# A graph network of four layers: the second layer's outputs turned in squares of 32 and through DRAM

## The chip, the cores and the metric

The kernel runs on one core of one Trainium2 chip. The time is device microseconds of one execution. The engines are called as in the profile: PE is TensorE, DVE is VectorE, ACT is ScalarE, POOL is GpSimd, SP is the engine that here only issues DMAs.

## What is computed

Four attention layers over a graph of 4096 nodes with 256 features each, all in float32. Every layer ends in a residual addition and a layer norm. The change concerns the second one:

```python
def _L1_gnn_ref(x, edge, Wq, bq, Wk, bk, Wv, bv):
    NHEAD, HEAD_DIM = 4, 64
    q = _split_heads(x @ Wq + bq)
    k = _split_heads(x @ Wk + bk)
    v = _split_heads(x @ Wv + bv)
    mask = (edge.T.astype(jnp.float32) - 1.0) * 10000.0
    scores = jnp.einsum('hnd,hmd->hnm', q, k) / np.sqrt(HEAD_DIM)
    scores = scores + mask[None, :, :]
    attn = jax.nn.softmax(scores, axis=-1)
    ctx = jnp.einsum('hnm,hmd->hnd', attn, v)
    return ctx.transpose(1, 0, 2).reshape(x.shape[0], NHEAD * HEAD_DIM)

x = _layernorm(x + _L0_gnn_ref(x, adj, L0_gnn_W, L0_gnn_a), axis=-1)
x = _layernorm(x + _L1_gnn_ref(x, adj, L1_gnn_Wq, ...), axis=-1)
x = _layernorm(x + _L2_gnn_ref(x, adj, L2_gnn_W, L2_gnn_a), axis=-1)
x = _layernorm(x + _L3_gnn_ref(x, adj, L3_gnn_Wq, L3_gnn_Wk), axis=-1)
```

The kernel computes the masked softmax without its division first: weights are exp(score) times the 0/1 mask, their products with the values are summed, and the sums are divided by the row sums of the weights at the end.

## The kernel before

The features X (4096 rows of 256) stay in SBUF through all four layers. Each layer walks over 8 blocks of 512 query nodes (`NB`, `QW`), and inside a block over the keys.

In the second layer (`multi_head_attention`) a block has 64 units (`NH`) of 64 keys. All four heads of a unit are held in one tile of 128x1024: two heads by partition halves, two by column halves. The loop at L1014 runs over all 8 x 64 units, with a lag of three units between scores and sums. One turn i of it does this:

- `scores` (L852): eight PE matmuls of the 64x64 quarter arrays write the scores of unit i to a PSUM tile `p` (L867; three such tiles, of two banks each), and ACT takes exp in place (L869). Every fourth unit four DMAs on SP fetch the masks of four units, 8 bits each (L860; three such mask buffers).
- `weights` (L871): DVE multiplies `p` by the mask into `prob` in SBUF (L879; eight such tiles). For the row sums, even units are added to `den` by a POOL addition (L889) and odd ones by a DMA issued on POOL that accumulates (L895); units 1 and 3 are copied there by DMAs on SP (L893). In four units of a block (`relief`) DVE does POOL's addition (L996).
- `sums` (L897): eight PE matmuls add the products of unit i-3 with its values to `acc`, two PSUM banks with one set of buffers (L903). In a block's last unit ACT copies the first bank to the SBUF tile `kept0` (L908) and DVE the second to `kept1` (L909), so that the next block can use `acc`. In that turn the sums are issued ahead of the scores (L1016).
- `finish(b - 1, j)` (L965): one step of the ending of the block before, where j = i - 3.

A block's results lie with features on partitions and nodes along the columns, and they have to be turned before they can be added to X. The steps of `finish` are: 7 and 9, DVE joins the three parts of `den` (L912); 12, PE sums `den` over partitions into a `p` tile (L925) and ACT copies that to `kept2` (L928); 15, PE turns the row sums (L933) and the first two of four row groups of the outputs (L940) into a `p` tile, DVE takes reciprocals (L948), multiplies (L954) and adds to X (L957); 18, PE turns the other two row groups and DVE does the same; 21 to 41, layer norm. `halves` (L959) takes the next of the three `p` tiles for each of steps 12, 15 and 18.

PE, DVE and ACT run in the order in which the program is written (`manual_schedule`, L1013). SP and POOL are ordered by the planner, by when it expects an instruction to be ready. The eighth block's ending is done by `tail` (L1027) in the third layer.

The last layer already has another way of turning (`squares_far`, L1192): DVE transposes 32x32 squares (L1197), four DMAs on SP write them to DRAM, one from each 32 partitions, in pieces of 32 elements (L1201), and one DMA on SP reads them back with nodes on partitions (L1204).

Of the kernel before, what the change touches and what calls it, by code (L numbers as in the profile page):

```python
# [9 lines left out]
FP = mybir.dt.float32  # L10
# [8 lines left out]
P = 128  # L19
D = 256  # L20
KC = D // P
QB = 4
QW = QB * P
# [5 lines left out]
def kernel(  # L29
# [27 lines left out]
    nc = tc.nc  # L57
    N = x.shape[0]
    NT = N // P
    NB = N // QW  # L60

    def pool(stack, name, bufs, **kw):
        return stack.enter_context(tc.tile_pool(name=name, bufs=bufs, reuse_waits="tile", **kw))
# [58 lines left out]
    def turning_apart(squares, far, part, to, eng, between=False):  # L122

        B = P // QB
        squares = squares.tile([P, QB, KC, P], FP, name="squares")
        for c in range(KC):
            if c and between:
                yield
            nc.vector.transpose(squares[:, :, c, :].rearrange("p q (k n) -> p k q n", n=B),
                                part(c).rearrange("p k (q f) -> p k q f", f=B))  # L130
        yield
        far = far.tile([QB, B, QB, KC * P], FP, name="far")
        eng.dma_start(far.rearrange("a f q m -> (a f) (q m)"), squares.rearrange("p q c m -> p (q c m)"))
        yield
        to = to()
        for q in range(QB):
            eng.dma_start(to[q * B:(q + 1) * B], far[:, :, q, :].rearrange("a f m -> f a m"))
        return to.rearrange("p a (c m) -> p c a m", c=KC)

    def block_turning(sb, once, dr, rows, eng):  # L140
        to = lambda: sb.tile([P, KC * QW], FP, name="xT").rearrange("p (a m) -> p a m", a=QB)
        return turning_apart(once, dr, lambda c: rows[:, :, c * P:(c + 1) * P], to, eng)

    def at_once(steps):
        while True:
# [587 lines left out]
    def multi_head_attention(w_sb, b_sb, tail, rows_of_den, rows_done, narrow_edges, ga):  # L733
# [8 lines left out]
        MJ = 4  # L742
        NH = N // d
        W = KC * QW
        kept, den, rden, mvs, roots = {}, {}, {}, {}, {}
        with ExitStack() as lay:
            keep = pool(lay, "mh_keep", 1)
            kT = keep.tile([P, KC, N], FP, name="kT")
            qT = keep.tile([P, KC, N], FP, name="qT")
            V = keep.tile([P, NH, P], FP, name="V")  # L750
# [146 lines left out]
            def sums(b, j):  # L897
                if j == 0:
                    acc[b] = [pa.tile([P, QW], FP, name=f"acc{c}") for c in range(KC)]
                for r in range(KC):  # L900
                    for c in range(KC):
                        half = slice(c * d, (c + 1) * d)
                        nc.tensor.matmul(acc[b][c][r * d:(r + 1) * d, :], V[half, j, r * d:(r + 1) * d],  # L903
                                         prob[b, j][half, r, :], start=(j == 0), stop=(j == NH - 1))
                if j == NH - 1:

                    kept[b] = [fin1.tile([P, QW], FP, name=f"kept{c}") for c in range(KC)]
                    nc.scalar.copy(kept[b][0], acc[b][0])  # L908
                    (nc.scalar.copy if b == NB - 1 else nc.vector.tensor_copy)(kept[b][1], acc[b][1])  # L909

            def join_sums(b, n, eng=nc.vector):
                eng.tensor_tensor(den[b][:, 0, :], den[b][:, 0, :], den[b][:, n, :], OP.add)  # L912
# [1 line left out]
            def row_sums(bank, b):  # L914


                kept[b].append(fin1.tile([P, QW], FP, name=f"kept{KC}"))
                pds = [bank() for _ in range(KC)]
                for r in range(KC):
                    for s in range(2):  # L920
                        for c in range(KC):
                            g = 2 * r + s
                            half = slice(c * d, (c + 1) * d)
                            lo = r * QW + s * QW // 2
                            nc.tensor.matmul(pds[c][g * G:(g + 1) * G, :QW // 2], ones[half, :G],  # L925
                                             den[b][half, 0, lo:lo + QW // 2], start=True, stop=True)
                for c in range(KC):
                    nc.scalar.copy(kept[b][KC][:, c * QW // 2:(c + 1) * QW // 2], pds[c][:, :QW // 2])  # L928

            def turned_row_sums(bank, b):  # L930
                pd = bank()
                for k in range(QB):
                    nc.tensor.transpose(pd[:, k * P:(k + 1) * P], kept[b][KC][:, k * P:(k + 1) * P], ident)  # L933
                return pd

            def turned_half(bank, b, k):
                po = bank().rearrange("p (k f) -> p k f", f=D)
                for i in range(2):
                    for c in range(KC):
                        nc.tensor.transpose(po[:, i, c * P:(c + 1) * P],  # L940
                                            kept[b][c][:, (k + i) * P:(k + i + 1) * P], ident)
                return po

            def reciprocals(pd, b):
                rden[b] = fin.tile([P, QB, H], FP, name="rden4")
                parts = pd.rearrange("p (c k r s g) -> p k c r s g", c=KC, k=2, r=KC, s=2)
                for s in range(2):
                    nc.vector.reciprocal(rden[b][:, 2 * s:2 * s + 2, :].rearrange("p k (c r) -> p k c r", c=KC),  # L948
                                         parts[:, :, :, :, s, 0])
# [9 lines left out]
            def halves():  # L959

                p = ps.tile([P, KC, QW], FP, name="p")
                left = [p[:, r, :] for r in range(KC)]
                return lambda: left.pop(0)

            def finish(b, j):  # L965

                rows = [X[:, b * QB + k, :D] for k in range(QB)]
                if j in (7, 9):
                    join_sums(b, j // 2 - 2)
                elif j == 12:  # L970
                    row_sums(halves(), b)
                elif j == 15:
                    bank = halves()
                    pd = turned_row_sums(bank, b)
                    po = turned_half(bank, b, 0)
                    reciprocals(pd, b)
                    half(po, b, 0)
                elif j == 18:
                    half(turned_half(halves(), b, 2), b, 2)
                elif j in (21, 23, 25, 27):  # L980
                    k = (j - 21) // 2
                    if k == 0:
                        mvs[b] = fin.tile([P, QB, 2], FP, name="mv")
                    one_row(mvs[b], k, rows[k])
                elif j == 29:
                    roots[b] = begin_root(mvs[b])
                elif j == 31:

                    end_root(*roots[b], nc.gpsimd)
                    lift_mean(mvs[b], *roots[b][:2], nc.gpsimd)  # L990
                elif j in (35, 37, 39, 41):
                    k = (j - 35) // 2
                    scale_row(rows[k], mvs[b], roots[b][1], k)
                if j + LAG - 1 in relief:

                    nc.vector.tensor_tensor(*late.pop(), OP.add)  # L996
                    ga.dots(b * QB + relief.index(j + LAG - 1), (1,) if b > 1 else (0, 1))
                elif j == 57:
                    ga.factors(b)
                elif j == 59 and b == 0:  # L1000
                    ga.sources(b)
                elif j == 63 and b == 1:
                    ga.row(0, nc.sync)
                elif j == 33 and b == NB - 2:
                    nc.gpsimd.dma_start(ga.first_mask, adjT.rearrange("(t p) i -> p t i", p=P)[:, :QB, :QW])
# [131 lines left out]
    def cosine_attention(co, tail):  # L1137
# [4 lines left out]
        with ExitStack() as lay:  # L1142
# [48 lines left out]

            def squares_far(b, h, both):  # L1192

                B = P // QB
                sq = fin1.tile([P, QW], FP, name=f"kept{h}").rearrange("p (a k c s) -> p a k c s", a=QB, k=2, c=KC)
                for n, quarter in enumerate(both):
                    nc.vector.transpose(sq[:, :, :, n, :].rearrange("p a k s -> p k a s"),  # L1197
                                        quarter.rearrange("p (k a r) -> p k a r", k=2, r=B))
                away = far.tile([B, QB, QW // P, QB, B], FP, name="away")
                for q in range(QB):  # L1200
                    nc.sync.dma_start(away[:, :, :, q, :].rearrange("r a m s -> r (a m) s"),  # L1201
                                      sq[q * B:(q + 1) * B].rearrange("r a k c s -> r (a k c) s"))
                t = (fin1 if h else cp).tile([P, QW], FP, name="kept2")
                nc.sync.dma_start(t, away.rearrange("r a m q s -> a r (m q s)"))  # L1204
                back[b, h] = t.rearrange("p (k f) -> p k f", k=2)

            def outputs_far(b, step, seen):
# [241 lines left out]
```

## Time and profile before

| | |
|---|---|
| median of 3 runs | 2770.95 us (2770.05 to 2772.3) |
| the profiled execution, whole | 2767.94 us |
| its span, first to last instruction | 2766.2 us |
| second layer's loop, from its first to its last block | about 795 to 1693 us of the span |
| from block to block in it (copies of L908) | 112.55 us, between the second and the third 114.41 |
| granted TensorE clock | 1.0 throughout |
| L940, transposes of outputs in the loop | 56, by fours: 8 in each of seven blocks |
| L954, L957 in the loop | 14 each, 689 to 700 ns |
| L889, additions on POOL | 220, 2536 ns in the mean |
| DMAs of L895 on POOL | 240 of 512 KB, 5.3 us to landing |
| DMA engines, share of time in a block | 0.89 to 0.92 |

A row of the page's groups or of the timeline reads: start and duration in us (timeline), engine, line of the program, operation, what it writes and reads, shapes, count, and in brackets how long the engine was idle before and what ended that. The chain of waits is followed back from the last instruction: each row is the work that had to end for the next to begin. PE's ends are modelled, so the chain's distances say more than PE's busy time.

### The profile page before, as it was taken

To read this page: it belongs to the slowest core of one execution; us is meant where nothing else is said; L and a number is where in the kernel's file an instruction comes from. 1 tells how busy PE (TensorE), PEld (TensorE's weight loads), DVE (VectorE), ACT (ScalarE), POOL (GpSimd) and SP (SyncE) were. 2 spreads that over 40 slices of the span, in tenths; PEclk is the share of its full clock that TensorE was granted. 3 is DMA by queue.
4 is the path that set the end of the run, shared out by engine and by line. 5 is a ranking of instruction groups with operands and counts; after the bars stand their busy time and mean duration, and the time that the engine had idled before them with its cause. 6 is when DMAs were issued, how large, how long until landed. Compare 5 with 4: busy or idle time off the path is not lost.

```text
span 2766.2 us, 50216 instructions
## 1 busy us (share of the span) xinstructions
PE 2750.6 (99%) x19365; PEld 1443.0 (52%) x19365; DVE 2307.0 (83%) x3145; ACT 1702.2 (62%) x2668; POOL 1077.0 (39%) x1020
## 2 busy tenths in 40 slices
PE   9999999999999999999999999999999999999999
PEld 5333333333543333333333336888888777777776
DVE  8899999999777788887888889888888876677776
ACT  7899999999346666666666665565655422222222
POOL 0000000000049878788788796454455000000000
PEclk9999999999999999999999999999999999999999
DMA  8798898987449899898998988578778544454442
GB/s 236 149 188 186 195 197 188 196 184 163 99 120 192 179 193 187 187 188 185 194 186 187 195 176 211 157 202 211 194 192 236 108 75 77 76 81 80 76 73 42
DMA packets 279673, 445.48 MB, mean 161 GB/s; under 512 B 55321, under 2 KB 156169, under 8 KB 274442
## 3 DMA queue, kind: packets, MB, share of 16 engines
q0 software_dynamic: 108784, 216.29, 46.9%
q1 hardware_dynamic: 164280, 218.88, 26.6%
q10 hardware_dynamic: 6370, 7.10, 0.8%
q8 instruction: 152, 2.49, 0.3%
q14 instruction: 87, 0.71, 0.1%
HBM read 335.94 MB, written 39.40 MB: 136 GB/s over the span
## 4 chain that ended last, share of the span: by engine, by line
PE 94%; DVE 4%; ACT 1%; issue 1%; POOL 0%; DVEq 0%; ACTq 0%; POOLq 0%
PE acc L475 26%; PE acc L333 19%; PE p L867 16%; PE acc L903 16%; PE p L1163 4%; PE g L1163 3%; PE g L777 2%; DVE prob L323 2%; PE acc L482 1%; ACT prob L309 1%; PE g L635 1%; PE g L1108 1%; PE pv L797 1%; PE acc L215 1%; PE g L348 0%
## 5 line engine op out<-in xcount | busy, mean ns | idle before, releaser
L879 DVE TENSOR_TENSOR prob<-p,mask 128x1024 f32<-128x1024 f32 x512 | 619.1, 1221 | 163.2 <-ACT p L869 158.6
L869 ACT ACTIVATE p<-p,shift 128x1024 f32<-128x1024 f32 x512 | 555.6, 1088 | 319.5 <-PE p L867 318.1
L333 PE MATMUL acc<-prob,V 128*32 128x512 f32 x5888 | 638.8, 593 | 1.9 <-DVE prob L323 1.8
L889 POOL TENSOR_TENSOR den<-den,prob 128x1024 f32<-128x1024 f32 x220 | 558.0, 2536 | 89.9 <-DVE prob L879 85.3
L309 ACT ACTIVATE prob<-row,dst 128x512 f32<-128x512 f32 x892 | 557.9, 711 | 3.0 <-PE acc L333 2.7
L867 PE MATMUL p<-qT,kT 64*64 64x512 f32 x4096 | 531.1, 590 | 2.3 <-DVE prob L879 2.3
L903 PE MATMUL acc<-prob,V 64*64 64x512 f32 x4096 | 529.9, 589 | 0.0
L323 DVE SCALAR_TENSOR_TENSOR prob<-prob,mask 128x2048 f32<-128x2048 f32 x224 | 504.8, 2282 | 17.2 <-ACT prob L309 16.9
L333 PEld LDWEIGHTS acc<-prob,V 128*32 128x32 f32 x5888 | 188.7, 110 | 435.9 <-issue 405.2
L475 PE MATMUL acc<-mix,mixed 128*128 128x256 f32 x1476 | 401.4, 380 | 1.9 <-DVE quarters L497 1.0
L903 PEld LDWEIGHTS acc<-prob,V 64*64 64x64 f32 x4096 | 157.4, 133 | 282.2 <-issue 280.3
L475 PEld LDWEIGHTS acc<-mix,mixed 128*128 128x128 f32 x1476 | 278.5, 190 | 45.8 <-PE acc L475 3.1
L867 PEld LDWEIGHTS p<-qT,kT 64*64 64x64 f32 x4096 | 154.2, 133 | 279.3 <-issue 252.3
L1176 DVE TENSOR_TENSOR prob<-prob,mask 128x1024 f32<-128x1024 f32 x128 | 156.3, 1221 | 142.9 <-ACT prob L1167 142.9
L895 POOL DMA_DIRECT2D den<-prob x240 | 233.3, 972 | 62.6 <-DMA den<-prob 27.6
L475 PE MATMUL acc<-prob,X 128*128 128x256 f32 x984 | 252.8, 379 | 0.7 <-ACT quarters L489 0.7
L1095 POOL DMA_DIRECT2D mask<-in_adjT x64 | 47.7, 745 | 527.9 <-DVE prob L1176 509.1
L475 PEld LDWEIGHTS acc<-prob,X 128*128 128x128 f32 x984 | 186.6, 190 | 80.1 <-issue 59.2
L608 DVE SCALAR_TENSOR_TENSOR prob<-r,own,mask 128x512 f32<-128x512 f32 x252 | 177.0, 743 | 49.0 <-POOL mix L467 12.2
L1167 ACT ACTIVATE prob<-p 128x512 f32<-128x512 f32 x144 | 86.1, 598 | 212.4 <-PE p L1163 212.4
L320 POOL DMA_DIRECT2D den<-prob x24 | 21.1, 878 | 483.7 <-DVE prob L314 461.6
L1167 ACT ACTIVATE prob<-g 128x512 f32<-128x512 f32 x112 | 66.9, 597 | 199.2 <-PE g L1163 199.2
(246 smaller groups left out, 3046.9 us busy)
## 6 DMA issues: line engine op xcount, KB each, us to landing
mask<-in_adjT SPq DMA_DIRECT2D x254, 512.0 KB
den<-prob POOLq DMA_DIRECT2D x240, 512.0 KB, 5.3
den<-prob POOLq DMA_DIRECT2D x32, 1024.0 KB, 9.3
mask<-edges SPq DMA_DIRECT2D x512, 64.0 KB
mask<-in_adjT POOLq DMA_DIRECT2D x64, 512.0 KB, 5.7
edges<-in_adj POOLq DMA_DIRECT2D x32, 512.0 KB, 17.1
far<-squares SPq DMA_DIRECT2D x16, 512.0 KB
den<-prob SPq DMA_DIRECT2D x16, 512.0 KB
```

The source lines that it names most:

```text
L309: nc.scalar.activation(z[:, h, :], r, AF.Relu, bias=-1.0, scale=dst[:, j, h:h + 1])
L323: nc.vector.scalar_tensor_tensor(z, z, 1.0, mask[m][:, j % MJ, :].unsqueeze(1).to_broadcast([P, H, QW]), OP.add, OP.mult)
L333: nc.tensor.matmul(acc[b][h * G:(h + 1) * G, n, :], part, prob[b, j][:, h, :], start=(j == 0), stop=(j == NT - 1 and n < HC))
L475: nc.tensor.matmul(acc[at][:, half * HW:(half + 1) * HW], w, a, start=(g == 0 and n in (0, 2, 3, 5)), stop=(g == NP - 1), skip_group_check ...
L608: nc.vector.scalar_tensor_tensor(z[:, n, :], r, ga.own[:, j:j + 1], mask[:, n, :], OP.add, OP.mult)
L867: nc.tensor.matmul(p[c * d:(c + 1) * d, r, :], kT[half, c, at:at + d], qT[half, c, cols], start=True, stop=True)
L869: nc.scalar.activation(p, p, AF.Exp, bias=shift)
L879: nc.vector.tensor_tensor(z, p, mask[m][:, j % MJ, :].unsqueeze(1).to_broadcast([P, KC, QW]), OP.mult)
L889: nc.gpsimd.tensor_tensor(to, to, flat, OP.add)
L895: nc.gpsimd.dma_start(to, flat, accum_op=OP.add)
L903: nc.tensor.matmul(acc[b][c][r * d:(r + 1) * d, :], V[half, j, r * d:(r + 1) * d], prob[b, j][half, r, :], start=(j == 0), stop=(j == NH - 1))
L1163: nc.tensor.matmul(p.rearrange("p (k i) -> p k i", k=QB), T[j // QB][:, 0, j % QB], T[b][:, 1], start=True, stop=True)
```

## The change

For the first seven blocks of the second layer the outputs are turned as in the last layer. At a block's end ACT still copies the first bank of `acc`; in place of the second copy DVE transposes the second bank's squares, in two halves of the columns, straight from PSUM into two tiles (`kept1`, `kept2`). At steps 1 and 2 of `finish` DVE transposes the squares of `kept0`, one half each, into the same two tiles, and SP is given four DMAs to DRAM and one back for each half. At step 15 only the row sums are turned by PE. At steps 17 and 19 DVE multiplies and adds as before, with the tile that came back from DRAM in the place of the PSUM tile. Step 18 is gone. The row sums take the name `kept0`. The eighth block is done as before. In the last layer the same instructions are now made by the shared functions.

```diff
--- before.py
+++ after.py
@@ -140,6 +140,25 @@
     def block_turning(sb, once, dr, rows, eng):
         to = lambda: sb.tile([P, KC * QW], FP, name="xT").rearrange("p (a m) -> p a m", a=QB)
         return turning_apart(once, dr, lambda c: rows[:, :, c * P:(c + 1) * P], to, eng)
+
+    def squares_of(t):
+        return t.rearrange("p (a k c s) -> p a k c s", a=QB, k=2, c=KC)
+
+    def turn_squares(sq, n, quarter):
+
+        nc.vector.transpose(sq[:, :, :, n, :].rearrange("p a k s -> p k a s"),
+                            quarter.rearrange("p (k a r) -> p k a r", k=2, r=P // QB))
+
+    def put_far(far, sq):
+        B = P // QB
+        away = far.tile([B, QB, QW // P, QB, B], FP, name="away")
+        for q in range(QB):
+            nc.sync.dma_start(away[:, :, :, q, :].rearrange("r a m s -> r (a m) s"),
+                              sq[q * B:(q + 1) * B].rearrange("r a k c s -> r (a k c) s"))
+        return away
+
+    def fetch(t, away):
+        nc.sync.dma_start(t, away.rearrange("r a m q s -> a r (m q s)"))
 
     def at_once(steps):
         while True:
@@ -742,9 +761,11 @@
         MJ = 4
         NH = N // d
         W = KC * QW
-        kept, den, rden, mvs, roots = {}, {}, {}, {}, {}
+        HW = QW // 2
+        kept, den, rden, mvs, roots, squares, back = {}, {}, {}, {}, {}, {}, {}
         with ExitStack() as lay:
             keep = pool(lay, "mh_keep", 1)
+            far = pool(lay, "mh_turned", 2, space=bass.MemoryType.DRAM)
             kT = keep.tile([P, KC, N], FP, name="kT")
             qT = keep.tile([P, KC, N], FP, name="qT")
             V = keep.tile([P, NH, P], FP, name="V")
@@ -904,9 +925,16 @@
                                          prob[b, j][half, r, :], start=(j == 0), stop=(j == NH - 1))
                 if j == NH - 1:
 
-                    kept[b] = [fin1.tile([P, QW], FP, name=f"kept{c}") for c in range(KC)]
+                    if b == NB - 1:
+                        kept[b] = [fin1.tile([P, QW], FP, name=f"kept{c}") for c in range(KC)]
+                        for c in range(KC):
+                            nc.scalar.copy(kept[b][c], acc[b][c])
+                        return
+                    kept[b] = [fin1.tile([P, QW], FP, name="kept0")]
                     nc.scalar.copy(kept[b][0], acc[b][0])
-                    (nc.scalar.copy if b == NB - 1 else nc.vector.tensor_copy)(kept[b][1], acc[b][1])
+                    squares[b] = [squares_of(fin1.tile([P, QW], FP, name=f"kept{1 + h}")) for h in range(2)]
+                    for h in range(2):
+                        turn_squares(squares[b][h], 1, acc[b][1][:, h * HW:(h + 1) * HW])
 
             def join_sums(b, n, eng=nc.vector):
                 eng.tensor_tensor(den[b][:, 0, :], den[b][:, 0, :], den[b][:, n, :], OP.add)
@@ -914,7 +942,7 @@
             def row_sums(bank, b):
 
 
-                kept[b].append(fin1.tile([P, QW], FP, name=f"kept{KC}"))
+                total = kept[b, "den"] = fin1.tile([P, QW], FP, name=f"kept{0 if b < NB - 1 else KC}")
                 pds = [bank() for _ in range(KC)]
                 for r in range(KC):
                     for s in range(2):
@@ -925,12 +953,12 @@
                             nc.tensor.matmul(pds[c][g * G:(g + 1) * G, :QW // 2], ones[half, :G],
                                              den[b][half, 0, lo:lo + QW // 2], start=True, stop=True)
                 for c in range(KC):
-                    nc.scalar.copy(kept[b][KC][:, c * QW // 2:(c + 1) * QW // 2], pds[c][:, :QW // 2])
+                    nc.scalar.copy(total[:, c * QW // 2:(c + 1) * QW // 2], pds[c][:, :QW // 2])
 
             def turned_row_sums(bank, b):
                 pd = bank()
                 for k in range(QB):
-                    nc.tensor.transpose(pd[:, k * P:(k + 1) * P], kept[b][KC][:, k * P:(k + 1) * P], ident)
+                    nc.tensor.transpose(pd[:, k * P:(k + 1) * P], kept[b, "den"][:, k * P:(k + 1) * P], ident)
                 return pd
 
             def turned_half(bank, b, k):
@@ -965,18 +993,21 @@
             def finish(b, j):
 
                 rows = [X[:, b * QB + k, :D] for k in range(QB)]
-                if j in (7, 9):
+                if j in (1, 2):
+                    h = j - 1
+                    turn_squares(squares[b][h], 0, kept[b][0][:, h * HW:(h + 1) * HW])
+                    away = put_far(far, squares[b][h])
+                    t = fin1.tile([P, QW], FP, name=f"kept{1 + h}")
+                    fetch(t, away)
+                    back[b, h] = t.rearrange("p (k f) -> p k f", f=D)
+                elif j in (7, 9):
                     join_sums(b, j // 2 - 2)
                 elif j == 12:
                     row_sums(halves(), b)
                 elif j == 15:
-                    bank = halves()
-                    pd = turned_row_sums(bank, b)
-                    po = turned_half(bank, b, 0)
-                    reciprocals(pd, b)
-                    half(po, b, 0)
-                elif j == 18:
-                    half(turned_half(halves(), b, 2), b, 2)
+                    reciprocals(turned_row_sums(halves(), b), b)
+                elif j in (17, 19):
+                    half(back.pop((b, (j - 17) // 2)), b, j - 17)
                 elif j in (21, 23, 25, 27):
                     k = (j - 21) // 2
                     if k == 0:
@@ -1191,17 +1222,11 @@
 
             def squares_far(b, h, both):
 
-                B = P // QB
-                sq = fin1.tile([P, QW], FP, name=f"kept{h}").rearrange("p (a k c s) -> p a k c s", a=QB, k=2, c=KC)
+                sq = squares_of(fin1.tile([P, QW], FP, name=f"kept{h}"))
                 for n, quarter in enumerate(both):
-                    nc.vector.transpose(sq[:, :, :, n, :].rearrange("p a k s -> p k a s"),
-                                        quarter.rearrange("p (k a r) -> p k a r", k=2, r=B))
-                away = far.tile([B, QB, QW // P, QB, B], FP, name="away")
-                for q in range(QB):
-                    nc.sync.dma_start(away[:, :, :, q, :].rearrange("r a m s -> r (a m) s"),
-                                      sq[q * B:(q + 1) * B].rearrange("r a k c s -> r (a k c) s"))
+                    turn_squares(sq, n, quarter)
                 t = (fin1 if h else cp).tile([P, QW], FP, name="kept2")
-                nc.sync.dma_start(t, away.rearrange("r a m q s -> a r (m q s)"))
+                fetch(t, put_far(far, sq))
                 back[b, h] = t.rearrange("p (k f) -> p k f", k=2)
 
             def outputs_far(b, step, seen):
```

## The prediction

> **What bounds the kernel now.** I read the page's busy table first, then the stretches of the second layer block by block, then the chain of waits inside one block, then the timeline around the instructions that the change touches.
>
> ```profile
> PE 2750.6 (99%) x19365; PEld 1443.0 (52%) x19365; DVE 2307.0 (83%) x3145; ACT 1702.2 (62%) x2668; POOL 1077.0 (39%) x1020
> ```
> ```profile
> 1131.00:1244.00 113.00, 113.00 (x1064) 40.62 (x1060) 93.46 (x99) 71.66 (x72) 92.47 (x65) 1.00 0.90 187
> ```
>
> TensorE (PE) is busy for 99% of the span; the second row is one block of the second layer (busy times in the order PE, weight loads, DVE, ACT, POOL, then granted clock, DMA share, GB/s). PE fills it; VectorE and GpSimd each have 20 us free in 113. A microsecond taken off PE here is a microsecond of the kernel, as long as no other engine makes PE wait.
>
> ```profile
> 932.41 0.86 PE p L867 x8
> 933.27 0.86 PE acc L903 x8
> 934.13 0.59 PE p L933 x4
> 934.72 0.44 PE p L940 x4
> 935.15 1.02 PE p L867 x8
> ...
> 940.46 0.59 PE p L940 x4
> 941.05 1.02 PE p L867 x8
> ```
>
> In the chain every unit of 64 keys is 0.86 us of scores and 0.86 of sums, 1.716 together; 64 of them are 109.85. The copies of L908 start 112.55 us apart in most blocks; the other 2.7 us are the three visits of the previous block's ending (steps 12, 15, 18), two of which are shown.
>
> **What it removes.** At step 15 four transposes of outputs (0.44 us); the four of the row sums stay and keep their start-up. At step 18 the whole visit: 0.59, and the 1.02 - 0.86 = 0.16 by which the scores after it are longer: 0.75. Together 1.19 us a block. Seven blocks change (the last keeps the old way): 7 x 1.19 = 8.3 us off PE. The trace has these transposes at 0.44 us for four, 0.11 each, as they overlap. [...]
>
> **What it adds on VectorE's half of the boundary.** The 0.68 us copy of acc1 (L909) becomes two transposes of 128x256 out of PSUM. No row shows that; L1197 transposes the same size out of SBUF in 0.43, a pair of them in 0.76, and the copy shows that reading PSUM costs 0.68 for 512 columns. Bounds 0.72 and 1.1; I take 0.8. The copy ended at 906.34 and PE's first sums into acc began at 906.59, so 0.25 us hide it: the loss is 0 to 0.17 a block, 0 to 1.2 in all. I take 0; with the cover gone each 0.1 us costs 0.7. At steps 1 and 2 a transpose of 0.43 joins a unit in which VectorE is busy 1.22 of 1.716: 1.65, which fits. Behind it waits the next mask multiplication (L879), with 1.55 us to spare (below). ACT keeps its copy of acc0.
>
> **What it adds on SP and the DMA engines.** Ten DMAs a block. The last layer does the same today:
>
> ```profile
> 2230.74 5.37 SPq L1201 DMA_DIRECT2D away<-kept  x6
> 2237.80 0.60 SPq L1204 DMA_DIRECT2D kept<-away  x1
> 2245.58 0.56 SPq L1204 DMA_DIRECT2D kept<-away  x1
> ```
>
> Eight writes at 0.63 us and two reads at 0.56 are 6.2 us of issuing. Each read waits on SP until its writes have landed, and from the first write to the end of the second read 15.4 us pass. POOL's queue gets none. Behind a read on SP are the mask loads; L879 waits for these. Three mask buffers of four units each mean that a mask is asked for when unit j ends and needed nine units later, 15.4 us. Where it queues behind both reads it is asked for about 15.4 - 3 x 1.716 = 10.3 us late; the four mask issues take about 2 and a landing about 5.3 (that of the den DMAs on the page), so it is between 8 us early and 2.2 us late. I take 0, as the first read goes out after 7 us and SP can issue masks before the second. The turned rows are wanted 16 and 18 units (27 and 31 us) after the first write, and the reads go out 7 and 15 us after it; with 5.3 for a landing 11 us or more cover them, and past that VectorE stands still. On the DMA engines the queue of these transfers took 27.7% of the 16 us from 2230, 4.4 us of all sixteen for all the writes and one read; 5.3 with the other. The block leaves 10% of 113, some 11 us, idle. I take 0 here too.
>
> **What it moves, and where I see the price.** The two multiplications by the reciprocals and the two additions to X (L954, L957) now run at steps 17 and 19, and their input is no longer PSUM but a tile in SBUF. So each has two inputs in SBUF. Today they ignore GpSimd:
>
> ```profile
> 935.97 2.35 POOL L889 TENSOR_TENSOR den<-den,prob 128x1024 f32<-128x1024 f32 x1 [0.34 <-DMA den<-prob]
> 936.03 0.70 DVE L954 TENSOR_TENSOR p<-p,rden 128x512 f32<-128x512 f32 x1
> 936.77 0.69 DVE L957 TENSOR_TENSOR X<-p,X 128x512 f32<-128x512 f32 x1
> ```
>
> With a PSUM input both take their 0.7 while L889 runs. VectorE instructions with two SBUF inputs don't:
>
> ```profile
> 1769.89 0.42 DVE L652 SCALAR_TENSOR_TENSOR e<-e,h 128x256 f32<-128x256 f32 x1
> 1770.12 0.77 POOL L466 TENSOR_TENSOR mix<-prob,mix 128x256 f32<-128x256 f32 x1 [2.60 <-DVE mix L465]
> 1770.34 0.83 DVE L653 TENSOR_TENSOR y<-X,e 128x256 f32<-128x256 f32 x1
> ...
> 1711.30 2.88 DVE L912 TENSOR_TENSOR den<-den 128x1024 f32<-128x1024 f32 x2
> 1711.45 1.64 POOL L466 TENSOR_TENSOR mix<-prob,mix 128x256 f32<-128x256 f32 x1 [0.62 <-DVE mix L465]
> ```
>
> L653 takes 0.42 where GpSimd rests and 0.83 here: GpSimd came during L652, went first when L652 ended, and L653 waited. Two L912 at 1.22 should take 2.4 and took 2.88, with L466 between them. So GpSimd, once waiting, goes between two such instructions of VectorE. [...]
>
> Steps 17 and 19 run in units 20 and 22, even units, and L889 is issued in every even unit: in the timeline it starts 0.16 us after the end of that unit's L879 (time t), as after 940.36 and 944.55. The multiplication starts before it, holds it until t + 0.60, and L889 then needs 2.22 more (at 921.42 it took 3.20 and ended 2.22 after an L912 that was ahead). The addition ends 0.56 later (a held L912 ended 1.09 after L889 instead of taking 1.22, so 0.69 - 0.13), and the next L879 1.12 after that: t + 4.50, instead of t + 1.716. What PE forgives shows where this happened once:
>
> ```profile
> 1033.12 2.96 POOL L889 TENSOR_TENSOR den<-den,prob 128x1024 f32<-128x1024 f32 x1
> 1033.74 3.43 DVE L912 TENSOR_TENSOR den<-den 128x1024 f32<-128x1024 f32 x1
> ...
> 1038.36 1.09 PE L867 MATMUL p<-qT,kT 64*64 64x512 f32 x8 [1.01 <-DVE prob L879]
> ```
>
> The unit's L879 should have ended at 1033.82 + 1.716 = 1035.54; the scores that wait for its buffer would have begun at 1035.45 + 1.716 = 1037.17, so 1.55 us are free (0.08 is the signal). Step 17 thus costs 4.50 - 1.716 - 1.55 = 1.23 us. Then L879 of unit 22 ends at t + 5.64, the second half goes the same way to t + 5.64 + 4.50 = t + 10.14, against 3 x 1.716 + 1.55 + 1.23 = 7.93: 2.21 more. Together 3.44 a block. Check: that third block lasted 114.41 instead of 112.55, 1.86 for one such wait; two would be 3.7. I take 3.45. Without the wait VectorE would be at most 1.3 us late, under the 1.55.
>
> **The sum.** 7 x (3.45 - 1.19) = +15.8 us on the profiled span of 2766.2: 2782.0, and 2783.7 with the 1.7 us that lie around it in that execution (2767.94). The median of the runs, 2770.95, stands 3 us above it, so 2787.
>
> **Rivals.** (1) *VectorE keeps the way to SBUF*, or GpSimd arrives over 1.3 us after t and finds both instructions done. Then 2770.95 - 8.3 = 2763, faster. For it: multiplication and addition are issued 0.06 us apart or overlapping, and DMA traffic may hold GpSimd back (it waited 27.6 us for den DMAs in 17 places). Against: every one of the 28 L653 into y took 0.83, and L889 starts 0.16 after t in every block at units 20 and 22. It decides once GpSimd's delay is over 1.3 us. (2) *Masks behind the reads on SP*, on top of the forecast: 2.2 x 7 = 15 us more, 2802. For it: DMA share 0.9, so writes may land later than in the last layer. Against: in the third block SP stood still for 11.5 us at its start, and the block lost 1.86 in all. (3) *Only one half of two is hit*: 7 x (1.23 - 1.19) = 0.3, 2771, no change.
>
> **Chances.** Forecast 66%, rival 1 17%, rival 2 13%, rival 3 4%. The likeliest has its own range of 2780 to 2794 (3.4 to 3.7 a block and 0 to 1.2 at the boundary, with some spread of runs). The range 2762 to 2802 takes in most of rival 1 and the nearer half of rival 2. Some 0.2% (5.5 us) is what a measurement here can tell: slower 0.79, same 0.04, faster 0.17.
>
> **What would show it.** Right: L954 at 0.7, L957 near 2.8 us in the seven blocks, L889 between them, PE idle behind L879 at units 24 and 26, blocks some 114.8 us apart; no L940 in them. Wrong: L957 at 0.7 and blocks 111.4 apart (rival 1); L879 waiting for mask DMAs at units 16 to 20 (rival 2). What fails first, if I am wrong, is the turn GpSimd takes between the two instructions.

## The result, and the profile after

The changed kernel takes 2856.88 us (median of 5 runs, 2852.89 to 2862.0) against 2770.05 (5 runs beside it, 2769.27 to 2772.3): 1.0314 times as long, 95% interval 1.0302 to 1.0326. The prediction was 2787, with a range of 2762 to 2802. The profiled execution took 2856.88 us, its span is 2855.1: 88.9 us more than the 2766.2 before, and 87.7 of them lie in the second layer's seven changed blocks. In the table below, "score interval n" is the time from the first score matmul of unit n of a block to that of unit n+1 (1.716 us undisturbed), summed over the seven blocks, after less before.

| score interval | after less before, 7 blocks | in one block, before and after |
|---|---|---|
| 14 | +57.2 us | 1.72, and 9.1 to 11.6 |
| 15, 16 | +14.2 | 2.42 for interval 15, and 4.0 to 4.7 |
| 23, 25 | +23.3 | 1.72 each, and 2.91 and 3.85 |
| 18, 21 | -8.0 | 2.85 and 2.41, and 2.41 and 1.72 |
| all others | +1.0 | |

So the seven blocks paid what the prediction priced (23.3 for the two additions to X, 8.0 saved), and 71 us that it had put at nothing. On the page and in the busy times of one block (granted clock, DMA share and GB/s are the last three columns) PE now stands still for 11 us of the block, and the clock is no longer 1.00:

```profile
PE 2761.0 (97%) x19309; PEld 1447.8 (51%) x19309; DVE 2344.1 (82%) x3166; ACT 1702.7 (60%) x2668; POOL 1086.4 (38%) x1020
```
```profile
1278.34:1402.83 124.49, 113.65 (x1048) 41.22 (x1044) 98.65 (x103) 71.24 (x72) 93.77 (x66) 0.97 0.86 177
1308.53:1315.36 6.83, 3.17 (x16) 0.80 (x16) 4.45 (x4) 1.09 (x1) 3.07 (x1) 0.50 0.41 95
```

**Interval 14.** In the timeline of that block, VectorE has finished unit 11 at 1301.32 and then waits 9.60 us for a mask DMA before it can multiply unit 12 (L900); PE stands still 7.88 us behind it.

```profile
1300.10 1.22 DVE L900 TENSOR_TENSOR prob<-p,mask 128x1024 f32<-128x1024 f32 x1
1310.91 1.22 DVE L900 TENSOR_TENSOR prob<-p,mask 128x1024 f32<-128x1024 f32 x1 [9.60 <-DMA mask<-edges]
```
```profile
1312.19 1.98 PE L888 MATMUL p<-qT,kT 64*64 64x512 f32 x8 [7.88 <-DVE prob L900]
```

The waits of L900 over the whole second layer say that it is so in every changed block (before the change, no mask DMA stands among them). In the first of the seven the profile names a write, `away<-kept`, for the 9.4 us; there too a load for units 12 to 15 landed at 931.84, and L900 began at 932.01:

```profile
its engine sat idle before it (us, times) until:
  ACT p L890: 144.6, 262
  DMA mask<-edges: 57.8, 7
  DMA away<-kept: 9.4, 1
```

SP's timeline shows which load it is. Three of the four loads for units 12 to 15 go out at 1287.87; the fourth is queued behind six writes, the first read and two writes, and goes out at 1300.85. It lands 10 us later, at 1310.79. From the first write to the end of the second read's issue 21.3 us pass (15.4 in the last layer).

```profile
1287.87 1.96 SPq L881 DMA_DIRECT2D mask<-edges  x3
1289.93 6.69 SPq L156 DMA_DIRECT2D away<-kept  x6
1297.96 0.56 SPq L161 DMA_DIRECT2D kept<-away  x1
1298.57 2.24 SPq L156 DMA_DIRECT2D away<-kept  x2
1300.85 6.34 SPq L881 DMA_DIRECT2D mask<-edges  x3
1310.64 0.58 SPq L161 DMA_DIRECT2D kept<-away  x1
```

**Interval 15.** The window 1308.53 to 1315.36 above has a granted clock of 0.50. It begins inside the stall and outlasts it by 3.2 us: PE's first eight score matmuls behind the stall take 1.98 us together, where eight took 1.07 ahead of it. Such a stretch comes with each of the seven stalls, for 6.83 or 10.24 us.

**Intervals 23 and 25** are the wait for GpSimd that the prediction forecast; the expectations below call it the lock. L982 (before: L954) takes 0.68, GpSimd's L910 comes, and L985 (before: L957), which took 0.69, takes 2.72 to 2.73 in all 14 cases:

```profile
1327.30 0.68 DVE L982 TENSOR_TENSOR kept<-kept,rden 128x512 f32<-128x512 f32 x1
1327.54 2.65 POOL L910 TENSOR_TENSOR den<-den,prob 128x1024 f32<-128x1024 f32 x1 [0.76 <-DVE prob L900]
1328.01 2.73 DVE L985 TENSOR_TENSOR X<-kept,X 128x512 f32<-128x512 f32 x1
...
1331.93 1.09 PE L888 MATMUL p<-qT,kT 64*64 64x512 f32 x8 [1.01 <-DVE prob L900]
```

### The profile page after: what moved, and what is told of

Read it like the earlier page. It is cut to its first block, busy times and chain, and to the rows that moved or that the text cites. A ratio compares the mean times of both kernels' runs of the same rounds, so it can differ in the third digit from the quotient of the medians.

```text
span 2855.1 us, 50229 instructions
## 1 busy us (share of the span) xinstructions
PE 2761.0 (97%) x19309; PEld 1447.8 (51%) x19309; DVE 2344.1 (82%) x3166; ACT 1702.7 (60%) x2668; POOL 1086.4 (38%) x1020
## 5 line engine op out<-in xcount | busy, mean ns | idle before, releaser
L900 DVE TENSOR_TENSOR prob<-p,mask 128x1024 f32<-128x1024 f32 x512 | 616.1, 1220 | 215.8 <-ACT p L890 144.6
L910 POOL TENSOR_TENSOR den<-den,prob 128x1024 f32<-128x1024 f32 x220 | 576.0, 2618 | 134.5 <-DVE prob L900 123.0
L888 PE MATMUL p<-qT,kT 64*64 64x512 f32 x4096 | 541.9, 598 | 78.9 <-DVE prob L900 78.9
L924 PE MATMUL acc<-prob,V 64*64 64x512 f32 x4096 | 538.6, 595 | 0.0
L924 PEld LDWEIGHTS acc<-prob,V 64*64 64x64 f32 x4096 | 163.9, 134 | 282.7 <-issue 281.9
L916 POOL DMA_DIRECT2D den<-prob x240 | 239.9, 1000 | 94.5 <-DVE prob L900 41.6
L339 POOL DMA_DIRECT2D den<-prob x24 | 21.1, 878 | 483.9 <-DVE prob L333 461.8
L484 DVE TENSOR_TENSOR mix<-prob 128x512 f32<-128x512 f32 x246 | 179.4, 729 | 7.9
```

The lines of the kernel that those rows point to most:

```text
L484: nc.vector.tensor_tensor(s[:, :2, :], z[:, 0, :].rearrange("p (h i) -> p h i", h=2), z[:, :, HW:], OP.subtract)
L888: nc.tensor.matmul(p[c * d:(c + 1) * d, r, :], kT[half, c, at:at + d], qT[half, c, cols], start=True, stop=True)
L900: nc.vector.tensor_tensor(z, p, mask[m][:, j % MJ, :].unsqueeze(1).to_broadcast([P, KC, QW]), OP.mult)
L910: nc.gpsimd.tensor_tensor(to, to, flat, OP.add)
L916: nc.gpsimd.dma_start(to, flat, accum_op=OP.add)
```

## The experiments

The first four runs take the two costs apart. "Halves" are the two pairs of L982 and L985.

**a_no_trip**: no DMA of the trip; the squares are added where they lie.

```diff
-                    away = put_far(far, squares[b][h])
-                    t = fin1.tile([P, QW], FP, name=f"kept{1 + h}")
-                    fetch(t, away)
-                    back[b, h] = t.rearrange("p (k f) -> p k f", f=D)
+                    back[b, h] = squares[b][h].rearrange("p a k c s -> p (a k c s)").rearrange("p (k f) -> p k f", f=D)
```

> Leaves out the trip through DRAM of the seven blocks (eight writes and two reads each): the two halves multiply and add the squares as VectorE left them, so outputs of the second layer are not in their places. Theory (the extra time is two things: some 9.5 us a block of waiting for masks that SP and the DMA queue bring late because of the trip, with the clock drop that follows it, and 3.3 us a block of the two additions that wait for GpSimd): only the second stays; blocks 114.7 us apart, scores late at units 24 and 26 by 1.2 and 2.1 as now, no clock drop, median 2770 + 7 x (3.3 - 1.2) = 2785. Rival (VectorE's four transposes a block, or the longer hold of the accumulator at the boundary, make masks and scores late): those are still there, so the waits at units 12 to 15 stay and the time is over 2830.

Measured: 2795.93 us, 1.0084 (1.0068 to 1.0101). No mask is waited for; intervals 23 and 25 are 2.90 and 3.85 in six of the seven blocks, as in the change. The undisturbed blocks last 114.83 us (the prediction's 112.55 + 3.45 - 1.19 = 114.81); others up to 116.96, with intervals 23, 24, 26 or 27 longer and three dips of the clock of 3.41 us. These make the seven blocks 20.4 us longer than before in the profiled execution, where the expectation had 14.7. The time is 11 us over the expectation; the rest of that lies between runs (the kernel before took 3 us more beside this run than beside the change). The trip is what costs the other 61 us.

**b_odd_steps**: the halves one turn earlier, in units 19 and 21, when GpSimd is inside an addition instead of about to start one.

```diff
-                elif j in (17, 19):
-                    half(back.pop((b, (j - 17) // 2)), b, j - 17)
+                elif j in (16, 18):
+                    half(back.pop((b, (j - 16) // 2)), b, j - 16)
```

> The changed kernel with the two halves at steps 16 and 18 instead of 17 and 19, that is in odd units, in which GpSimd is given no addition. Theory (an addition of GpSimd goes between VectorE's multiplication and addition, and only that costs): the multiplication waits some 0.9 us for the rest of the addition of the unit before, the second instruction takes 0.7; VectorE is then at most 1.4 us late, under the 1.55 that are free, and the 3.3 us a block go: 2857 - 23 = 2834. Rival (two times 1.4 us more on VectorE within three units are too much whatever GpSimd does): 2850 or more.

Measured: 2844.52 us, 1.0262 (1.0247 to 1.0278). The stalls at 23 and 25 are gone, 0.7 us at interval 24 is left. Now the multiplication is what waits (0.81 in the first half, 2.00 in the second), and every addition takes 0.69. The stall at interval 14 stays (9.7 to 12.3). The time is 10 us over the 2834 of the theory: the profile has 5.0 of them at interval 24 and 3.4 at interval 14.

**c_ahead**: masks asked for eight units earlier in the program. (`ask` holds the four loads that stood in `scores`.)

```diff
+                n = b * NH + j
                 if j % MJ == 0:
...
+                    for u in range(0, 3 * MJ, MJ) if n == 0 else (n + 2 * MJ,):
+                        if u < len(units):
+                            ask(*units[u])
```

> The changed kernel with each group of masks asked for eight units earlier in the program, so that the planner puts all four loads of the fourth group ahead of the writes on SP; the fourth load of the fifth group then stands behind the second read. Theory A (the order on SP: one load of the fourth group behind eight writes and a read): the 9.5 us a block at unit 12 go, the fifth group comes in time or at most 2 us late, 2857 - 66 = 2791 to 2805. Theory B (the writes' packets are slow to drain beside the den DMAs, and whatever stands behind them on the queue is late): the wait moves to unit 16 and keeps half of its size or more, 2820 or more.

Measured: 2883.28 us, 1.0402 (1.0386 to 1.0417), worse. All loads for units 12 to 15 are now ahead of the writes, and interval 14 is 1.72; but three of the loads for units 16 to 19 are behind the first read and the fourth is behind the second, and interval 18 is 11.8 to 16.7. What stands behind the trip is late, whichever group it is.

**h_ahead_later_odd**: c_ahead, the reads written at steps 8 and 10, the halves at 16 and 18.

> Masks asked for eight units earlier, the reads given to SP at steps 8 and 10 instead of 1 and 2, so that the fifth group of masks is ahead of both, and the halves at steps 16 and 18. Theory (late masks and GpSimd's addition are all that the change costs): what is left is the work taken off PE, 1.2 us in each of seven blocks, 2770 - 8 = 2762. Rival (the trip loads the DMA engines so that den DMAs or masks come late in any order): 2770 or more, with VectorE or GpSimd waiting for DMAs.

Measured: 2824.37 us, 1.0187 (1.0172 to 1.0202). Interval 22 is now the long one, 5.2 to 10.4 us; in two blocks interval 18 is 4.5 and 4.7. The order alone doesn't mend it: the loads land late. In the fourth changed block the four loads for units 20 to 23 go out right behind the two reads, at 1297.88 to 1299.36, and land at 1311.5 to 1312.1; VectorE waits for them from 1307.91 to 1312.24.

The next four asked why. The trip writes 4,096 pieces of 128 bytes a block. **i_512** keeps the number of the DMAs and their order in the program and writes pieces of 512 bytes; the features come back in another order within a row, which the views of the two additions undo.

```diff
-        away = far.tile([B, QB, QW // P, QB, B], FP, name="away")
+        away = far.tile([B, QB, QB, P], FP, name="away")
         for q in range(QB):
-            nc.sync.dma_start(away[:, :, :, q, :].rearrange("r a m s -> r (a m) s"),
-                              sq[q * B:(q + 1) * B].rearrange("r a k c s -> r (a k c) s"))
+            nc.sync.dma_start(away[:, :, q, :], sq[q * B:(q + 1) * B].rearrange("r a k c s -> r a (k c s)"))
...
+        nc.sync.dma_start(t, away.rearrange("r a q m -> a r (q m)"))
```

> The pieces of the writes are 512 bytes long instead of 128 (1,024 a block instead of 4,096, as many DMAs, in the same places); the order of the features within a row is straightened by views of the two additions and a copy of the reciprocals. Theory D, the small pieces are slow to drain beside the row sums' accumulations and everything behind them on the queue is late: the trip takes 12 us or less instead of 20.7, the masks of the fourth group land nearly in time, score interval 14 falls from 9-11.6 us to 4 or less, no stretch at half clock follows, and the time is about 2795 (2785 to 2808), the stalls of about 1.2 and 2.1 us at intervals 23 and 25 staying. Theory E, what counts is the number of DMAs and their order (eight writes and two reads ahead of the masks, each with its issue and its place among the few that may be under way): interval 14 stays over 7 us and the time over 2835.

Measured: 2871.19 us, 1.0357 (1.0332 to 1.0382). Theory D falls. (The stall is at interval 18, 12.2 to 14.3 us: the planner put all loads for units 12 to 15 ahead of the reads here, and those for 16 to 19 behind both.)

**j_512_all** (i_512 with the orders of h_ahead_later_odd, halves at 16 and 20) and **o_512_odd** (i_512, halves at 16 and 20):

> Pieces of 512 bytes, masks asked for eight units earlier, reads at steps 8 and 10, halves at steps 16 and 20. Theory D: no mask is late, intervals 23 and 25 are near 1.72, and the time is about 2768 (2760 to 2778), so equal to the kernel before or a little faster. Theory E: a stall of 5 us or more remains in each block, as it did with the small pieces at interval 22, and the time is near 2820.

> The 512-byte pieces with the order of the change, and the halves at steps 16 and 20. Theory D and the lock together: run i_512 less 7 x (1.2 + 2.1 - 0.7) = 18, so about 2777 (2768 to 2790). Theory E: run b_odd_steps, 2844, within 10.

Measured: 2840.92 us, 1.0238 (1.0223 to 1.0253), and 2851.8, 1.0278 (1.0263 to 1.0293). Both keep the stall, at interval 18 (10.4 to 16.3 us, and 12.1 to 13.8). Theory E's numbers held to 21 and 8 us, but it gave no reason why a load should take 10 us to land.

**e_no_trip_odd**: a_no_trip with the halves of b_odd_steps.

> The trip left out (the second layer's outputs are added unturned across partitions), the halves at steps 16 and 18: neither the masks nor the addition of GpSimd stand in the way. If mask lateness and the lock are all that the change costs, this is the kernel before less what TensorE is spared: run a_no_trip, 2796, less 7 x 2.6 = 18, less its dips, about 2772 (2762 to 2780), no score interval over 3.5 us. A third cost that neither explains would show as a time over 2785.

Measured: 2769.81 us, 0.9988 (0.9979 to 0.9998), blocks of 112.16 to 112.18 us but for one (114.67; 114.41 before). Without the trip, and with 0.7 us a block of the wait for GpSimd left at interval 24, the change is worth 0.1%; no third cost is there.

The reason was in the packets and landings of the traces so far. While a read runs (in the change, until 2 us behind the issue of the next mask load, so that no other packets of this size mix in), we can count how many of its 2,048-byte packets are under way at one time:

```
packets of a read under way at once              most      mean while any is   us, first to last
after, first read of the 7 blocks                5 to 7    3.3 to 4.0          1.4 to 3.4
i_512, the same, whole                           6         2.8 to 3.9          4.1 to 4.9
before, the last layer's 14 reads                5 to 7    3.0 to 4.0          2.9 to 4.0
u_512_flat (below), first read of the 7 blocks   15 to 20  6.0 to 10.8         1.1 to 1.9
```

and when the sixteen parts of a DMA land, for three DMAs of SP's queue in the block shown above (the two writes behind the first read, and the mask load that VectorE waited for):

```
twelve parts                 the other four
1303.81 to 1304.26           1307.05 to 1310.19
1304.21 to 1304.90           1309.89 to 1310.57
1304.54 to 1305.16           1310.08 to 1310.79
```

The read's own semaphore shows it most directly. A write or a mask load counts sixteen landings. Each of the 28 such reads in the change's trace, and each of the 14 in the trace before, has five counts: one about 1 us behind its issue, and four landings (1306.65 to 1307.70 for the first read of the block shown). In u_512_flat and p_read4 below, the second layer's reads count sixteen.

So we take a read of 256 KB to lie on four of the sixteen DMA engines, 32 of its 128 packets of 2,048 bytes on each, among the row sums' packets of 4,096 bytes (about 340 ns each); the traces do not name a packet's engine. The three DMAs above, which lie behind the read and count sixteen, have twelve parts within 0.45 to 0.69 us of each other and their last part 6.25 to 6.38 us behind their first. In these runs the count goes with the read's outermost dimension: 4 quarters in `fetch`, with four landings; 128 rows in u_512_flat and 32 in p_read4, with sixteen. No run shows more of what sets the count.

**u_512_flat** changes that dimension alone: i_512 with the quarter ahead of the row in DRAM, so that the read's outermost dimension is 128 rows.

```diff
-        away = far.tile([B, QB, QB, P], FP, name="away")
+        away = far.tile([QB, B, QB, P], FP, name="away")
...
-            nc.sync.dma_start(away[:, :, q, :], sq[q * B:(q + 1) * B].rearrange("r a k c s -> r a (k c s)"))
+            nc.sync.dma_start(away[:, :, q, :].rearrange("a r m -> r a m"), sq[q * B:(q + 1) * B].rearrange("r a k c s -> r a (k c s)"))
...
-        nc.sync.dma_start(t, away.rearrange("r a q m -> a r (q m)"))
+        nc.sync.dma_start(t, away.rearrange("a r q m -> (a r) (q m)"))
```

> Run i_512 with one thing changed, as many DMAs of the same sizes in the same order: the tensor in DRAM holds the quarter ahead of the row, so that the read has 128 rows in one run as its outermost dimension instead of four quarters. Theory F, of the traces so far: never more than 4 or 5 of the read's 2,048-byte packets are under way at once, and a third of the other DMAs' sixteen parts, four of them, land 4 to 7 us after the other twelve; so each read runs on 4 of the 16 DMA engines, 32 packets of about 110 ns on each, between the accumulations' packets of 340 ns, and what lies behind it on those four is late. Then the read's packets are under way 12 to 16 at once, the four late parts go, the stall at score interval 18 falls from 12 us to under 4, and the time is about 2805 (2790 to 2825). Theory E, the number of DMAs and their order on the queue: 2871, within 8, with the stall as it was.

Measured: 2812.06 us, 1.0153 (1.0139 to 1.0167): 59 us less than i_512 for a change of the address order (57 by the two ratios), with the DMAs in the same order on SP. The read is spread (last row of the table). The waits of the mask multiplication over the layer, i_512 first and u_512_flat second:

```profile
  ACT p L901: 127.5, 241
  DMA mask<-edges: 91.7, 8
```
```profile
  ACT p L901: 142.8, 260
  DMA mask<-edges: 23.9, 6
```

What is left comes from the order on SP. In u_512_flat's timeline the loads for units 16 to 19 are behind the second read, which waits until 1293.3 for its writes to land:

```profile
1285.59 0.34 SPq L168 DMA_DIRECT2D kept<-away  x1
1285.97 2.07 SPq L164 DMA_DIRECT2D away<-kept  x2
1293.34 0.34 SPq L168 DMA_DIRECT2D kept<-away  x1
1293.72 17.76 SPq L892 DMA_DIRECT2D mask<-edges  x16
```

**p_read4**: the change with each read cut into four DMAs of 32 rows.

```diff
-        nc.sync.dma_start(t, away.rearrange("r a m q s -> a r (m q s)"))
+        for a in range(QB):
+            nc.sync.dma_start(t[a * P // QB:(a + 1) * P // QB], away[:, a].rearrange("r m q s -> r (m q s)"))
```

> The change as it was (128-byte pieces) with each read cut into four DMAs of 32 rows, one for each quarter: eight reads a block instead of two. Theory F: each of the four is spread over all sixteen engines, the stalls at score intervals 14 and 15 fall from 10 us together to under 4, and the time is 2800 to 2830. Theory E: six DMAs more a block ahead of the masks, so not better than 2857, about 2875.

Measured: 2843.47 us, 1.0267 (1.0253 to 1.0281): better than the change, as theory F has it, but short of its numbers; interval 14 is 7.2 to 9.6 us. In the fourth changed block the load for units 12 to 15 that comes last goes out 14.1 us after the first write (10.9 in the change), as the first four reads hold SP for 4.5 us, and is there in 4, all sixteen parts within 1 us of each other (10 in the change). So the landing gained 6 us and the issuing lost 3: interval 14 is 2.4 shorter there (7.39 for 9.81). F and E each have a part here.

**v_512_flat_odd** (u_512_flat, halves at 16 and 20) and **x_512_flat_all** (with masks asked for earlier and reads at steps 8 and 10 as well):

> u_512_flat with the halves at steps 16 and 20. Theory F and the lock: u_512_flat less 7 x 2.6 = 18, about 2785 (2768 to 2805). Theory E: as o_512_odd, 2852, within 8.

> v_512_flat_odd with masks asked for eight units earlier and reads at steps 8 and 10. Theory F: with the engines even and the masks ahead no stall over 1 us is left, and the time is about 2768 (2760 to 2785), equal to the kernel before or a little under it. Theory E: as j_512_all, 2841, within 8.

Measured: 2787.37 us, 1.0064 (1.0052 to 1.0077), as theory F has it, and 2778.32, 1.0029 (1.0018 to 1.0041), 10 us over its 2768. Of the 86.8 us, x_512_flat_all has 78.6 back. One long stall is left in it, at interval 18 of the second changed block (7.8 us), and interval 26 is 2.9 long in six blocks.

**z1_all_16_18** (x with the halves at 16 and 18) and **z3_reads_behind** (x with the reads queued behind the loads for units 16 to 19, halves at 18 and 20) looked for the rest:

```diff
-                    fetch_rows(t, aways.pop((b, h)))
+                    with tc.issue_after(asked[b + 1, 4].ins):
+                        fetch_rows(t, aways.pop((b, h)))
```

> x_512_flat_all with the halves at steps 16 and 18. If what was left there is GpSimd's addition ahead of the second half's product (2.79 us in place of 0.68; intervals 22 and 26 together 1.7 us long in every block), 0.7 remains of it as in e_no_trip_odd: x_512_flat_all less 7 x 1.0, so about 2771 (2766 to 2775), with the one stall of 6 us in the second turned block still there. If the spread of the reciprocals and the turned views cost it, no change: 2778.

> x_512_flat_all with the two reads behind the mask loads for units 16 to 19 on SP's queue, and the halves at steps 18 and 20. If the stall left in the second turned block is those masks behind the reads, which wait for the writes to land, no score interval is over 3.5 us in any block, the half clock does not appear, and the time is 2763 to 2772: the kernel before or up to 0.2% less. If the masks are late for another reason (the writes themselves, or too few places under way), an interval of 5 us or more stays in that block and the time is 2772 or more.

Measured: 2786.61 us, 1.005 (1.0037 to 1.0063), and 2782.11, 1.0031 (1.0019 to 1.0043). z1 misses: interval 26 is short again, but 24 is 3.15 in six blocks (2.41 to 2.43 in e_no_trip_odd), and the stall at interval 18 of the second changed block grew to 10.2. In z3 that interval is 3.2, so those masks were late for their place behind the reads. But another of 5.5 us came at 24 in the same block: the loads for units 20 to 23 are behind the reads now and come 2.3 us late, and then both instructions of the first half wait for GpSimd (1.73 for 0.68, and 3.36 for 0.69):

```profile
1055.61 2.36 DVE L917 TENSOR_TENSOR prob<-p,mask 128x1024 f32<-128x1024 f32 x2 [2.34 <-DMA mask<-edges]
1057.88 1.73 DVE L1014 TENSOR_TENSOR kept<-kept,by_parts 128x512 f32<-128x512 f32 x1
1059.64 3.36 DVE L1017 TENSOR_TENSOR X<-kept,X 128x512 f32<-128x512 f32 x1
```

In the other six blocks of each the product of a half waits for GpSimd; in z3, with the halves in units 21 and 23, it takes 1.72 to 2.02 us for 0.68:

```profile
1287.75 1.72 DVE L1014 TENSOR_TENSOR kept<-kept,by_parts 128x512 f32<-128x512 f32 x1
1289.50 0.69 DVE L1017 TENSOR_TENSOR X<-kept,X 128x512 f32<-128x512 f32 x1
...
1292.38 2.00 DVE L1014 TENSOR_TENSOR kept<-kept,by_parts 128x512 f32<-128x512 f32 x1
```

No version that turns the rows beats the kernel before. The best that was measured for the idea is e_no_trip_odd's 0.1%, with the trip left out; the 8.0 us taken off PE would be 0.3%, which no run shows.

## Why the prediction was wrong

**Right, with its sizes.** "So GpSimd, once waiting, goes between two such instructions of VectorE": 14 times of 14. 3.45 us a block were forecast (1.23 and 2.21), 3.3 came (1.19 at interval 23 and 2.14 at 25). "Together 1.19 us a block" off PE: 8.0 of the 8.3. The boundary: the two transposes out of PSUM took 0.77 us together (0.8 forecast), and PE lost nothing. VectorE's additions did not find the turned rows late.

**The step that failed** is the one on SP and the DMA engines: "it is between 8 us early and 2.2 us late. I take 0", and "On the DMA engines ... I take 0 here too". That is rival 2's mechanism, at unit 12 instead of 16 to 20, and at 8.2 us a block (10.2 with the half clock behind it) instead of 2.2. Two of its numbers were wrong. The landing of a mask load was taken as 5.3 us, from DMAs on another queue; behind a read it was 10. And the DMA engines were taken as one pool, 5.3 us of work against 11 idle, while each read, going by its four landings, lay on four of them. The trace before could have shown it: in its last layer such reads have 5 to 7 packets under way at most, and four landings each. And as to the order, "SP can issue masks before the second" read was so, but one load in four of a group was put behind the first, and 0.5 us before it was needed. Both parts count: with the landing of 4.3 us that such a load had in p_read4, the wait of 9.6 us in the block shown would still be some 3.8, by an estimate.

**The term that was absent** is the half clock: each stall of PE (7 to 10 us) brought 6.83 or 10.24 us at a granted clock of 0.50, the first 3.41 of them still inside the stall; intervals 15 and 16 behind it are 14 us longer in all. With it the sum closes: 57.2 + 14.2 + 23.3 - 8.0 + 1.0 = 87.7.

## What to carry to other kernels

For each DMA that is added, count how many parts it lands in, not only its bytes: here a read whose outermost dimension was 4 landed in four, and the loads behind it, which land in sixteen, had 6.25 to 6.38 us between their first part and their last in the block shown. With 128 and 32 outermost the reads landed in sixteen, and u_512_flat took 59 us less than i_512. And see which loads the queue now issues behind a wait: in the block shown the fourth load for units 12 to 15 went out at 1300.85, 13 us behind the first. A stall on a TensorE that is otherwise busy for 99% of the time can also cost more than its length: each of the seven stalls of 7 to 10 us brought 6.83 or 10.24 us at a clock of 0.50, and intervals 15 and 16 behind them were 14.2 us longer in all.

## What the runs showed of the hardware

- DMAs that count sixteen landings landed in twelve parts and four where a read that counts four was ahead: the mask load shown has 6.2 us between its first and its last part, the same load in p_read4, where the reads count sixteen, 0.4.
- Pieces of 512 bytes for 128 gained nothing in i_512, where a read has at most 6 packets under way (2871 for 2857, with the mask loads in another order on SP).
- The lengths of the half clock were 3.41, 6.83, 10.24, 13.65 and (once, in c_ahead) 17.07 us, multiples of one step, and within a run its beginnings lie whole steps apart: in the change's trace the second to the seventh begin 37, 74, 111, 147, 184 and 220 steps of 3.413 us behind the first, at 929.65.
- We cut the traces of the 14 runs in which the clock fell ahead of the end into steps of 3.41 us on this grid. Of 11,346 steps at full clock, 78 were followed by half clock: those in which PE's records cover up to 0.43 of the time (one of them, at 0.425, was not), and none with 0.455 or more. In the change's trace these are 8 of 817, with 0 to 0.24; of the others there the least covered has 0.455. In u_512_flat half clock came with a stall of 1.96 us (from 1077.43). Of the steps at half clock in the 14 traces, each with less than 0.79 of busy PE was followed by half clock and each from 0.86 on by full clock; in the change's trace the bounds are 0.79 and 0.93. PE's ends are modelled, so these bounds are approximate.
- Of two instructions of VectorE with both inputs in SBUF, the one that waits for GpSimd depends on the turn: in the change the addition (2.72 for 0.69), as GpSimd's addition is begun during the multiplication; in b_odd_steps the multiplication (2.00 for 0.68), as it is already under way.
